# A sequential graph dilation on one core: columns written as turns of the updated rows, and row counts taken from the nearer end

## The chip, the cores and the metric

The kernel runs on one core of one Trainium2 chip. The metric is the time of one execution on the device in microseconds (us); of the kernel before there are three runs. One further execution was recorded by the hardware profiler, and all durations below come from it.

## The reference

Sixteen graphs of 1024 nodes with 128 features pass four graph layers, each followed by a residual add and a layer norm. The change touches only the dilation at the start of the second layer. It walks over the rows of a symmetric 0/1 adjacency and thins each row out; what one row loses, its column loses too, so later rows see what earlier ones did:

```python
def step(carry, n):
    row = jnp.take(carry, n, axis=0)
    nbi = row.astype(jnp.int32)
    num = jnp.sum(nbi)
    sf = jnp.where(num > T_DIL, (num + K_DIL - 1) // K_DIL, 1)   # T_DIL 10, K_DIL 2
    rank = jnp.cumsum(nbi)
    rm = row & (rank % sf == 0)
    valid = (mask_b[n] != 0) & (num > 1)
    rm = jnp.where(valid, rm, False)
    keep = ~rm
    carry = carry.at[n].set(row & keep)
    carry = carry.at[:, n].set(carry[:, n] & keep)
    return (carry, None)
```

A row with more than ten neighbours loses those whose rank is a multiple of half the row's count, rounded up: the middle one, and the last too where the count is even. The thinned adjacency then serves three mean aggregations (SAGE layers); the other three layers use the full one. The mask is all ones in these inputs.

## The kernel before, in words

`fast_kernel` computes the four layers, with tests whose failure sets a flag; a second, general kernel stands behind the flag. In the dilation all sixteen adjacencies lie in SBUF as fp8 (`Y[b]`, 8 row tiles of 128 by 1024 columns, held four matrices to a tile `Yq`). They go in two groups of eight (GB = 8), each prepared in two halves of four (QB = 4). A step is one row tile k of one group g, and there are 16, in the order k, g. A step has three parts:

- `prepare` (from L1033): for each half, VectorE cuts the upper triangle of the diagonal block (`uY`, L1048) and adds up row blocks (`front`, `back`, L1052 to L1058: the sum of three of the first four blocks, or of all four for k of 4 and up, in bf16). TensorE counts into the PSUM tile `s0` (L1066), with the adjacency's column block as the stationary operand and constants (`twos`, `step0`) as the moving one: it gives twice the number of neighbours before a column, and the row's total in column 0. VectorE then makes `sk` (L1069) and small rows: `v1m`, `l1`, `past` (L1070 to L1076).
- `fixed_point` (from L1081): rows of one tile influence each other through the diagonal block. Six evaluations (EVALS = 6) settle how much each row has lost: VectorE marks the hits in `mid` (L1097), TensorE sums them over the rows into `pd` (L1100), VectorE takes the new total `ti` (L1104) and its threshold `thr` (L1092). At the end the diagonal blocks are corrected (L1113) and the per-row numbers `negc` and `wid` made (L1117 to L1130).
- `removal` (from L1132), once for each of the eight members: TensorE counts ranks over the row in two halves of 512 columns, each in its own PSUM bank `s` (L1143). The constant `step`, a triangle of 128 columns followed by 512 twos, is the moving operand; the upper half starts from `front` (and block k where `front` lacks it). ScalarE turns each half into the distance from the middle, `q` (L1145, an absolute value with `negc` as its bias). VectorE compares it with the half width `wid` to get `keep` (L1147) and clears the row by a bitwise and (L1148). Last the column: TensorE copies it in by the identity (L1153) and adds the turned `keep` (L1156), half by half in PSUM `pc`, and ScalarE writes the column back as the positive part of the sum less one (L1157).

The order: `fixed_point` of a step is issued in turns with the `removals` of the step before, an evaluation and then a member, and after four removals half of the `prepare` of the same group's next row tile. The framework's scheduler lays out each engine's queue from this at compile time, and may take ready work of a later part ahead; each engine then runs its queue in order and waits where an operand or a buffer is missing. In the recorded order the rank counts of later members run ahead of the columns of earlier ones. PSUM has eight banks of 512 fp32 columns, all in use here: two for `s0`, one for `pd`, three for `s`, two for `pc`. `q` and `keep` have two buffers, the small rows three. The first four halves are prepared before the loop; the last removals have no evaluation beside them. The stores of matrices 0 to 7 (L1159) close the stage, and the next layer loads them back.

Of the kernel before, what the change touches and what calls it, by code (L numbers as in the profile page):

```python
# [9 lines left out]
F32 = mybir.dt.float32  # L10
F16 = mybir.dt.float16
F32R = mybir.dt.float32r
BF16 = mybir.dt.bfloat16
I32 = mybir.dt.int32
# [625 lines left out]
def fast_kernel(ctx: ExitStack, tc: tile.TileContext, t: dict, out: bass.AP, flag: bass.AP):  # L640
# [221 lines left out]
    step = consts.tile([P, P + 512], BF16, name="step")  # L862
    nc.vector.memset(step, 2.0)
    nc.vector.scalar_tensor_tensor(step[:, :P], upper, 2.0, identb, op0=OP.mult, op1=OP.add)

# [5 lines left out]
    twos = step[:, P:]  # L871
# [3 lines left out]
    off = consts.tile([P, NT, B], F32, name="off")  # L875
    nc.vector.tensor_scalar(off, mok.rearrange("p (b k) -> p k b", k=NT), -1.0, 1.0e5, op0=OP.add, op1=OP.mult)
# [140 lines left out]
    with ExitStack() as ph:  # L1017
        sb = ph.enter_context(tc.tile_pool(name="dl_sb", bufs=2, reuse_waits="tile"))
        small = ph.enter_context(tc.tile_pool(name="dl_small", bufs=3, reuse_waits="tile"))
        ps_b = ph.enter_context(tc.tile_pool(name="dl_pb", bufs=2, space=PSUM, reuse_waits="tile"))  # L1020
        ps_d = ph.enter_context(tc.tile_pool(name="dl_pd", bufs=1, space=PSUM, reuse_waits="tile"))
        ps_s = ph.enter_context(tc.tile_pool(name="dl_ps", bufs=3, space=PSUM, reuse_waits="tile"))
# [8 lines left out]
        def prepare(st, k, g):  # L1031
# [6 lines left out]

            st.front = sb.tile([P, GB, P], BF16, name="front", bufs=3)
            if st.with_last:  # L1040
                st.last = sb.tile([P, GB, P], FP8, name="last")
            for q in range(GB // QB):
# [7 lines left out]
                front = st.front[:, qs, :]  # L1050
                kf = [kb for kb in range(4) if kb != k]
                nc.vector.tensor_tensor(front, Yg[:, :, kf[0], ks], Yg[:, :, kf[1], ks], op=OP.add)  # L1052
                if k < 4:
                    nc.vector.tensor_tensor(front, front, Yg[:, :, kf[2], ks], op=OP.add)
                else:
                    back = sb.tile([P, QB, P], BF16, name="back")
                    nc.vector.tensor_tensor(back, Yg[:, :, kf[2], ks], Yg[:, :, kf[3], ks], op=OP.add)
                    nc.vector.tensor_tensor(front, front, back, op=OP.add)  # L1058
                s0 = ps_b.tile([P, QB, P], F32, name="s0")
                for i in range(QB):  # L1060
                    terms = [(Y[b0 + i][:, kb, ks], P if kb <= k else 1, step0 if kb == k else None)
                             for kb in range(4 if k >= 4 else 0, NT)]
                    if k >= 4:
                        terms.insert(0, (front[:, i, :], P, None))
                    for j, (y, n, m) in enumerate(terms):
                        nc.tensor.matmul(s0[:, i, :n], y, twos[:, :n] if m is None else m,  # L1066
                                         start=(j == 0), stop=(j == len(terms) - 1))
# [686 lines left out]
```

## Time and profile before

| What | us |
|---|---|
| median of three runs (lowest, highest) | 2961.86 (2958.01, 2962.2) |
| the profiled execution's own time | 2964.0 |
| its span, first to last instruction | 2962.2 |
| first evaluation of the dilation starts | 696.2 |
| removals and evaluations together, until the last column is written | about 708 to 1102 |
| end of the evaluations of the first step, of the last | 708.6, 1078.2 |
| busy over the span: TensorE, VectorE, ScalarE | 2725.4, 2196.2, 2024.2 |

The profile's lines are read like this. In a stretch, the busy time of an engine is the time in which at least one of its instructions is in work; a pipelined engine looks busy until the last result is out. A group line names the line of code, engine, operation, output and inputs, shapes and count; behind it stand the summed busy time and the mean of one in ns, and after a second bar the idle time of that engine just before these instructions, with what ended it. A wait is put down to what came last. Consecutive instructions of one engine overlap a little, so an instruction's place in its queue is the distance to the next start and not its duration.

### The profile page before, as it was taken

How to read it: one execution, taken by the hardware profiler on the slowest of the kernel's cores; microseconds unless marked ns; L12 is line 12 of the kernel's file. 1: busy time of each engine (PE TensorE's matmuls, PEld its weight loads, DVE VectorE, ACT ScalarE, POOL GpSimd, SP SyncE). 2: the span in 40 equal slices, each digit the busy share in tenths (PEclk: the TensorE clock that was granted, in tenths of full speed). 3: DMA queues.
4: the chain of work that ended last, by engine and by line, in shares of the span. 5: the costliest groups of instructions: out<-in, count | busy, mean ns of one | idle time of the engine just before them, and what ended most of it. 6: DMA issues, size and time to landing. Idle time of an engine off the chain costs nothing.

```text
span 2962.2 us, 42088 instructions
## 1 busy us (share of the span) xinstructions
PE 2725.4 (92%) x14771; PEld 1695.2 (57%) x14834; DVE 2196.2 (74%) x6087; ACT 2024.2 (68%) x3476; POOL 325.8 (11%) x295
## 2 busy tenths in 40 slices
PE   7999999996999889999899988999999999999996
PEld 3444444443666657877788873555555555555554
DVE  5777777777999976776688785777777777776765
ACT  6788888874788786666555435666666667676753
POOL 0000000030000001111122230001000101000000
PEclk9999999997999999999999997999999999999998
DMA  5444444420000052233467681111111111111000
GB/s 187 135 157 151 163 163 157 151 91 16 2 2 2 2 195 82 100 107 136 162 212 266 228 327 50 47 62 64 61 68 69 60 58 57 57 57 57 22 15 23
DMA packets 124125, 297.91 MB, mean 101 GB/s; under 512 B 12672, under 2 KB 65664, under 8 KB 116736
## 3 DMA queue, kind: packets, MB, share of 16 engines
q1 hardware_dynamic: 103440, 211.65, 21.6%
q0 software_dynamic: 20464, 83.47, 7.1%
q8 instruction: 119, 1.95, 0.3%
q14 instruction: 102, 0.84, 0.1%
HBM read 211.04 MB, written 84.02 MB: 100 GB/s over the span
## 4 chain that ended last, share of the span: by engine, by line
PE 36%; issue 19%; DVE 17%; POOL 4%; ACT 4%; DMA 2%; SPq 0%; POOLq 0%; DVEq 0%; ACTq 0%
PE ph L1550 8%; PE acc L1306 7%; PE ph L766 5%; PE acc L1626 4%; PE ph L1410 3%; PE pmm L724 3%; POOL ln_rstd L745 2%; PE ph L759 2%; DVE ln_st L794 2%; PE ph L1536 2%; DVE em L1612 2%; ACT xn L801 2%; POOL rn L745 1%; DVE A L1679 1%; PE acc L981 1%
## 5 line engine op out<-in xcount | busy, mean ns | idle before, releaser
L724 PE MATMUL pmm<-G,hT 128*128 128x512 f32 x1024 | 512.8, 614 | 10.7 <-DVE mx L1612 6.7
L801 ACT ACTIVATE xn<-xn,ln_nb,ln_rstd 128x128 f32<-128x128 f32 x512 | 207.4, 481 | 112.9 <-DVE ln_nb L799 112.8
L724 PEld LDWEIGHTS pmm<-G,hT 128*128 128x128 f32 x1024 | 175.0, 193 | 166.7 <-issue 118.3
L745 POOL TENSOR_TENSOR ln_rstd<-ln_rstd,mhalf 128x8 f32<-128x8 f32 (+1 forms) x68 | 115.9, 1704 | 1323.9 <-DVE nmx L1614 606.7
L1306 PE MATMUL acc<-a,lo 128*128 128x512 f32 x768 | 243.5, 401 | 15.5 <-DVE lo L1273 15.5
L1626 PE MATMUL acc<-em,hs 128*128 128x512 f32 x512 | 251.8, 611 | 3.5 <-DVE hs L1623 1.9
L981 PE MATMUL acc<-em,hs 128*128 128x512 f32 x512 | 245.7, 601 | 6.5 <-DVE hs L978 5.6
L1306 PE MATMUL acc<-a,hi 128*128 128x512 f32 x768 | 244.1, 402 | 3.7 <-ACT hi L1272 3.5
L1145 ACT ACTIVATE q<-s,negc 128x512 f16<-128x512 f32 x256 | 170.6, 697 | 59.2 <-DVE negc L1124 22.3
L1143 PE MATMUL s<-step,carry 128*128 128x384 bf16 (+3 forms) x1034 | 199.4, 304 | 7.9 <-DVE carry L1113 3.2
L1157 ACT ACTIVATE carry<-pc,negone 128x512 fp8e4<-128x512 f32 x256 | 166.8, 699 | 38.3 <-PE pc L1156 28.9
L972 DVE CUSTOM_DVE_ANT_0 em<-pmm,msk 128x1024 f32<-128x1024 f32 x128 | 155.9, 1218 | 40.6 <-PE acc L981 20.3
L1306 PEld LDWEIGHTS acc<-a,lo 128*128 128x128 f32 x768 | 144.4, 190 | 54.8 <-DVE lo L1273 21.1
L1612 DVE CUSTOM_DVE_ANT_0 em<-pmm,msk 128x1024 f32<-128x1024 f32 x128 | 155.6, 1216 | 25.9 <-PE acc L1626 21.3
L922 ACT ACTIVATE carry<-an 128x1024 fp8e4<-128x1024 f32 x128 | 134.4, 1050 | 50.7 <-DMA an<-in_adj 50.5
L1306 PEld LDWEIGHTS acc<-a,hi 128*128 128x128 f32 x768 | 143.0, 190 | 37.1 <-ACT hi L1272 4.0
L1607 ACT ACTIVATE msk<-A,nbig 128x1024 bf16<-128x1024 fp8e4 x128 | 145.9, 1140 | 26.6 <-DVE mx L1612 23.4
L974 ACT ACTIVATE em<-em,mx 128x1024 f32<-128x1024 f32 x128 | 146.0, 1141 | 25.4 <-DVE mx L972 22.7
L981 PEld LDWEIGHTS acc<-em,hs 128*128 128x128 f32 x512 | 90.9, 189 | 123.9 <-issue 87.2
L1410 PE MATMUL ph<-Wx,hT 128*128 128x128 f32 x768 | 153.4, 282 | 3.0 <-ACT nT L1435 1.4
L1410 PE MATMUL ph<-Wr,ag 128*128 128x128 f32 x768 | 151.1, 279 | 1.4 <-DMA ag<-ag_d 1.2
L1666 ACT CAST A<-A 128x1024 fp32r<-128x1024 fp8e4 x64 | 64.2, 1040 | 124.8 <-PE ph L1550 124.6
(294 smaller groups left out, 6181.9 us busy)
## 6 DMA issues: line engine op xcount, KB each, us to landing
an<-in_adj SPq DMA_DIRECT2D x128, 512.0 KB, 3.5
adj_d<-carry POOLq DMA_DIRECT2D x16, 1024.0 KB, 4.2
A<-dil_d SPq DMA_DIRECT2D x16, 1024.0 KB, 7.1
rdeg<-rdeg_d SPq DMA_DIRECT2D x32, 512.0 KB, 4.2
ag_d<-ag POOLq DMA_DIRECT2D x32, 512.0 KB, 5.3
ag<-ag_d SPq DMA_DIRECT2D x32, 512.0 KB, 6.3
A<-adj_d SPq DMA_DIRECT2D x16, 1024.0 KB, 4.7
xn<-in_x SPq DMA_DIRECT2D x16, 512.0 KB, 4.2
```

The lines of the kernel that those rows point to most:

```text
L724: nc.tensor.matmul(p[:, h * 512:(h + 1) * 512], lhsT, rhs[:, h * 512:(h + 1) * 512], start=True, stop=True)
L745: nc.gpsimd.tensor_tensor(r, r, mhalf[:, :n], op=OP.pow)
L801: nc.scalar.activation(r[:, k.start + i, :], r[:, k.start + i, :], AF.Identity, scale=rstd[:, i:i + 1], bias=nb[:, i:i + 1])
L981: nc.tensor.matmul(s.acc[:, c], hs, em[:, c], start=(jt == 0), stop=(jt == NT - 1))
L1143: nc.tensor.matmul(s[:, lo or 0:], y, twos if lo is None else step[:, :512 - lo], start=(j == 0), stop=(j == len(terms) - 1))
L1145: nc.scalar.activation(q[:, h * 512:(h + 1) * 512], s, AF.Abs, bias=st.negc[:, i:i + 1])
L1157: nc.scalar.activation(Y[b][:, hb, ks], pc, AF.Relu, bias=negone, saturate=False)
L1306: nc.tensor.matmul(acc, part[:, jt, :], pieces[h * NT // 2 + i][:, j, :], start=(jt == 0 and p == 0), stop=(jt == NT - 1 and p == 1))
L1410: nc.tensor.matmul(p[:, i * P:(i + 1) * P], x[:, j * P:(j + 1) * P], W, start=(n == 0), stop=(n == 1))
L1550: nc.tensor.matmul(p, part[:, jt, :], A[:, jt, c], start=(jt == 0 and i == 0), stop=(jt == NT - 1 and i == 1))
L1612: nc.vector.tensor_tensor_reduce(em, e, msk, 1.0, 0.0, op0=OP.add, op1=OP.max, accum_out=mx)
L1626: nc.tensor.matmul(s.acc[:, c], hs, em[:, c], start=(jt == 0), stop=(jt == NT - 1))
```

## The change

- Rank counts of the upper half start at the row's far end: four matmuls of 512, 384, 256 and 128 columns, as in the lower half, with a reversed triangle that is put behind the twos in `step`. ScalarE turns the count around with scale -1 and a second bias, `posc`, which holds `negc` plus twice the row's total `v`. `front` and `back` with all their adds go, and `prepare` counts every block by a matmul of its own.
- A column is made from the updated row: seven matmuls turn the row's other blocks with twice the identity as the moving operand, and only the diagonal block k is still copied in and joined by the turned `keep`. All nine results lie in one `pc` tile of two banks, and one ScalarE instruction of 1024 columns writes the whole column.
- `off`, the term that switches masked rows off (zero here), becomes bf16 and goes into `l1` in one instruction; `v1m` is made from `l1` once for a group, at the start of `fixed_point`; `thr` isn't made anew after the evaluations; `past` is corrected by `off` at the very end.
- PSUM: `s0` has one buffer instead of two, `s` two instead of three, `pc` two of two banks each instead of two of one.

```diff
@@ -859,21 +859,24 @@
     upper8 = consts.tile([P, P], FP8, name="upper8")
     nc.vector.tensor_copy(upper8, upper, saturate=False)
-    step = consts.tile([P, P + 512], BF16, name="step")
+    step = consts.tile([P, P + 512 + P], BF16, name="step")
     nc.vector.memset(step, 2.0)
     nc.vector.scalar_tensor_tensor(step[:, :P], upper, 2.0, identb, op0=OP.mult, op1=OP.add)
+    nc.vector.tensor_scalar(step[:, P + 512:], step[:, :P], -1.0, 2.0, op0=OP.mult, op1=OP.add)
+    identb2 = consts.tile([P, P], BF16, name="identb2")
+    nc.vector.tensor_scalar(identb2, identb, 2.0, None, op0=OP.mult)
     step0 = consts.tile([P, P], BF16, name="step0")
     nc.vector.tensor_copy(step0, step[:, :P])
     nc.vector.memset(step0[:, 0:1], 2.0)
     onec = consts.tile([P, 1], BF16, name="onec")
     nc.vector.memset(onec, 1.0)
-    twos = step[:, P:]
+    twos = step[:, P:P + 512]
     negone = consts.tile([P, 1], F32, name="negone")
     nc.vector.memset(negone, -1.0)
-    off = consts.tile([P, NT, B], F32, name="off")
-    nc.vector.tensor_scalar(off, mok.rearrange("p (b k) -> p k b", k=NT), -1.0, 1.0e5, op0=OP.add, op1=OP.mult)
+    off = consts.tile([P, NT, B], BF16, name="off")
+    nc.vector.tensor_scalar(off, mok.rearrange("p (b k) -> p k b", k=NT), -1.0, 1.0e4, op0=OP.add, op1=OP.mult)
@@ -1017,9 +1020,9 @@
     with ExitStack() as ph:
         sb = ph.enter_context(tc.tile_pool(name="dl_sb", bufs=2, reuse_waits="tile"))
         small = ph.enter_context(tc.tile_pool(name="dl_small", bufs=3, reuse_waits="tile"))
-        ps_b = ph.enter_context(tc.tile_pool(name="dl_pb", bufs=2, space=PSUM, reuse_waits="tile"))
+        ps_b = ph.enter_context(tc.tile_pool(name="dl_pb", bufs=1, space=PSUM, reuse_waits="tile"))
         ps_d = ph.enter_context(tc.tile_pool(name="dl_pd", bufs=1, space=PSUM, reuse_waits="tile"))
-        ps_s = ph.enter_context(tc.tile_pool(name="dl_ps", bufs=3, space=PSUM, reuse_waits="tile"))
+        ps_s = ph.enter_context(tc.tile_pool(name="dl_ps", bufs=2, space=PSUM, reuse_waits="tile"))
         ps_c = ph.enter_context(tc.tile_pool(name="dl_pc", bufs=2, space=PSUM, reuse_waits="tile"))
         def words(v):
@@ -1035,8 +1038,6 @@
             st.sk = sb.tile([P, GB, P], F16, name="sk")
             st.v1m = small.tile([P, GB], F32, name="v1m")
             st.l1 = small.tile([P, GB], F32, name="l1")
-
-            st.front = sb.tile([P, GB, P], BF16, name="front", bufs=3)
             if st.with_last:
                 st.last = sb.tile([P, GB, P], FP8, name="last")
             for q in range(GB // QB):
@@ -1047,33 +1048,17 @@
                 uY = sb.tile([P, QB, P], FP8, name="uY")
                 nc.vector.tensor_tensor(words(uY), words(Yg[:, :, k, ks]),
                                         words(upper8)[:, None, :].to_broadcast([P, QB, P // 4]), op=OP.bitwise_and)
-                front = st.front[:, qs, :]
-                kf = [kb for kb in range(4) if kb != k]
-                nc.vector.tensor_tensor(front, Yg[:, :, kf[0], ks], Yg[:, :, kf[1], ks], op=OP.add)
-                if k < 4:
-                    nc.vector.tensor_tensor(front, front, Yg[:, :, kf[2], ks], op=OP.add)
-                else:
-                    back = sb.tile([P, QB, P], BF16, name="back")
-                    nc.vector.tensor_tensor(back, Yg[:, :, kf[2], ks], Yg[:, :, kf[3], ks], op=OP.add)
-                    nc.vector.tensor_tensor(front, front, back, op=OP.add)
                 s0 = ps_b.tile([P, QB, P], F32, name="s0")
                 for i in range(QB):
-                    terms = [(Y[b0 + i][:, kb, ks], P if kb <= k else 1, step0 if kb == k else None)
-                             for kb in range(4 if k >= 4 else 0, NT)]
-                    if k >= 4:
-                        terms.insert(0, (front[:, i, :], P, None))
-                    for j, (y, n, m) in enumerate(terms):
-                        nc.tensor.matmul(s0[:, i, :n], y, twos[:, :n] if m is None else m,
-                                         start=(j == 0), stop=(j == len(terms) - 1))
+                    for kb in range(NT):
+                        m = step0 if kb == k else twos[:, :P if kb < k else 1]
+                        nc.tensor.matmul(s0[:, i, :m.shape[1]], Y[b0 + i][:, kb, ks], m, start=(kb == 0), stop=(kb == NT - 1))
                 l1 = st.l1[:, qs]
                 nc.vector.tensor_tensor(st.sk[:, qs, :], s0, uY, op=OP.mult)
-                nc.vector.tensor_scalar(st.v1m[:, qs], s0[:, :, 0], 0.5, -1.0, op0=OP.mult, op1=OP.add)
-                nc.vector.tensor_scalar(l1, s0[:, :, 0], -1.0, None, op0=OP.add)
+                nc.vector.scalar_tensor_tensor(l1, s0[:, :, 0], -1.0, off[:, k, gs], op0=OP.add, op1=OP.add)
                 if not st.with_last:
                     nc.vector.tensor_tensor(past[:, k, gs], l1, s0[:, :, P - 1], op=OP.subtract)
-                nc.vector.tensor_add(st.v1m[:, qs], st.v1m[:, qs], off[:, k, gs])
-                nc.vector.tensor_add(l1, l1, off[:, k, gs])
                 if st.with_last:
                     nc.vector.tensor_tensor(st.last[:, qs, :], st.sk[:, qs, :], per_member(l1), op=OP.is_equal, saturate=False)
                 yield
@@ -1085,6 +1070,7 @@
             st.negc = negc = small.tile([P, GB], F32, name="negc")
             st.wid = wid = small.tile([P, GB], F32, name="wid")
             v1m, l1 = st.v1m, st.l1
+            nc.vector.tensor_scalar(v1m, l1, 0.5, -0.5, op0=OP.mult, op1=OP.add)
             ti = small.tile([P, GB], I32, name="ti")
             nc.vector.tensor_copy(ti, v1m)
             for e in range(EVALS):
@@ -1115,13 +1101,13 @@
             v = small.tile([P, GB], F32, name="v")
             nc.vector.tensor_sub(v, l1, ti)
-            thr = small.tile([P, GB], I32, name="thr")
-            nc.vector.tensor_scalar(thr, ti, 1, None, op0=OP.bitwise_or)
             hw = small.tile([P, GB], F32, name="hw")
-            nc.vector.tensor_tensor(hw, thr, ti, op=OP.is_equal)
+            nc.vector.tensor_tensor(hw, thr, prev, op=OP.is_equal)
             nc.vector.tensor_sub(negc, hw, v)
             nc.vector.scalar_tensor_tensor(hw, v, 0.5, hw, op0=OP.mult, op1=OP.mult)
             nc.vector.tensor_sub(negc, negc, hw)
+            st.posc = posc = small.tile([P, GB], F32, name="posc")
+            nc.vector.scalar_tensor_tensor(posc, v, 2.0, negc, op0=OP.mult, op1=OP.add)
             en = small.tile([P, GB], F32, name="en")
             mk = mok[:, g * GB * NT + k:(g + 1) * GB * NT:NT]
             nc.vector.scalar_tensor_tensor(en, v, 10.5, mk, op0=OP.is_gt, op1=OP.mult)
@@ -1136,25 +1122,25 @@
             q = sb.tile([P, N], F16, name="q")
             for h in range(H2):
                 s = ps_s.tile([P, 512], F32, name="s")
-                terms = [(Y[b][:, kb, ks], max((kb - 4 * h) * P, 0)) for kb in range(4 * h, 4 * h + 4)]
-                if h:
-                    terms = [(st.front[:, i, :], None)] + [(Y[b][:, k, ks], None)] * (k < 4) + terms
-                for j, (y, lo) in enumerate(terms):
-                    nc.tensor.matmul(s[:, lo or 0:], y, twos if lo is None else step[:, :512 - lo],
-                                     start=(j == 0), stop=(j == len(terms) - 1))
-                nc.scalar.activation(q[:, h * 512:(h + 1) * 512], s, AF.Abs, bias=st.negc[:, i:i + 1])
+                for j in range(4):
+                    y, w = Y[b][:, 4 * h + (3 - j if h else j), ks], 512 - j * P
+                    if h:
+                        nc.tensor.matmul(s[:, :w], y, step[:, step.shape[1] - w:], start=(j == 0), stop=(j == 3))
+                    else:
+                        nc.tensor.matmul(s[:, j * P:], y, step[:, :w], start=(j == 0), stop=(j == 3))
+                nc.scalar.activation(q[:, h * 512:(h + 1) * 512], s, AF.Abs, scale=-1.0 if h else 1.0,
+                                     bias=(st.posc if h else st.negc)[:, i:i + 1])
             keep = sb.tile([P, N], FP8, name="keep")
             nc.vector.tensor_scalar(keep, q, st.wid[:, i:i + 1], None, op0=OP.not_equal, saturate=False)
             nc.vector.tensor_tensor(words(Y[b][:, k, :]), words(Y[b][:, k, :]), words(keep), op=OP.bitwise_and)
-            for h in range(H2):
-                hb = slice(4 * h, 4 * h + 4)
-                pc = ps_c.tile([P, 4, P], F32, name="pc")
-                nc.tensor.matmul(pc, identb, Y[b][:, hb, ks], start=True, stop=False)
-                for j in range(4):
-                    c = (4 * h + j) * P
-                    nc.tensor.matmul(pc[:, j, :], keep[:, c:c + P], identb, start=False, stop=(j == 3))
-                nc.scalar.activation(Y[b][:, hb, ks], pc, AF.Relu, bias=negone, saturate=False)
+            pc = ps_c.tile([P, NT, P], F32, name="pc")
+            nc.tensor.matmul(pc[:, k, :], identb, Y[b][:, k, ks], start=True, stop=False)
+            nc.tensor.matmul(pc[:, k, :], keep[:, ks], identb, start=False, stop=True)
+            for j in range(NT):
+                if j != k:
+                    nc.tensor.matmul(pc[:, j, :], Y[b][:, k, j * P:(j + 1) * P], identb2, start=True, stop=True)
+            nc.scalar.activation(Y[b][:, :, ks], pc, AF.Relu, bias=negone, saturate=False)
             if k == NT - 1 and b < B // 2:
                 nc.gpsimd.dma_start(dil8_d[b], Y[b].bitcast(F32))
@@ -1710,6 +1696,7 @@
         nc.vector.tensor_tensor(mok, mok, mf, op=OP.not_equal)
         nc.vector.tensor_scalar(zeros, zeros, 0.5, None, op0=OP.is_lt)
+        nc.vector.tensor_sub(past, past, off[:, :NT - 2, :])
         nc.vector.tensor_scalar(past, past, 0.5, None, op0=OP.is_lt)
         nc.vector.tensor_scalar(nodeg, nodeg, 0.5, None, op0=OP.is_lt)
         bms = sb.tile([P, 7], F32, name="bms")
```

## The prediction

> **What bounds the kernel now.** I read the summary page first, then the busy time by stretch, since the change touches one stage of about 394 us (708 to 1102 us) in a span of 2962.2. Columns: length, busy time and instruction count of each engine, granted TensorE clock, DMA share, GB/s.
>
> ```profile
> core 0: us, PE busy (x) PEld busy (x) DVE busy (x) ACT busy (x) POOL busy (x), PEclk, DMA share, GB/s
> 708.00:800.00 92.00, 88.05 (x986) 57.43 (x1004) 84.59 (x245) 72.01 (x116) 0.00 (x0) 0.98 0.01 2
> 800.00:1000.00 200.00, 190.61 (x2105) 124.52 (x2134) 194.69 (x569) 163.62 (x267) 0.00 (x0) 1.00 0.01 2
> 708.00:1102.00 394.00, 369.23 (x4081) 242.51 (x4147) 365.94 (x1054) 315.32 (x514) 4.30 (x8) 0.98 0.09 33
> ```
>
> VectorE is at 97% from 800 to 1000 and 93% over the stage; TensorE looks as busy, but its busy time includes the latency of every burst. So VectorE is the first limit, TensorE close behind, ScalarE at 80% third. Next the groups of instructions inside 708 to 1101 (busy sum and mean duration before the bar's second half, idle before them after it):
>
> ```profile
> L1145 ACT ACTIVATE q<-s,negc 128x512 f16<-128x512 f32 x256 | 170.6, 697 | 59.2 <-DVE negc L1124 22.3 <-PE s L1143 17.2 <-DVE ti L1104 12.8
> L1157 ACT ACTIVATE carry<-pc,negone 128x512 fp8e4<-128x512 f32 x254 | 165.4, 698 | 38.3 <-PE pc L1156 28.9 <-DVE front L1052 3.7 <-DVE ti L1104 2.7
> L1097 DVE TENSOR_TENSOR mid<-sk,thr 128x1024 fp8e4<-128x1024 f16 x90 | 109.7, 1219 | 0.7
> L1156 PE MATMUL pc<-identb,keep 128*128 128x128 bf16 x1020 | 99.1, 220 | 0.5 <-DVE keep L1147 0.4
> L1153 PE MATMUL pc<-carry,identb 128*128 128x512 fp8e4 x256 | 97.2, 380 | 7.2 <-DVE carry L1148 4.2 <-ACT carry L1157 0.9
> ...
> L1147 DVE TENSOR_SCALAR keep<-q,wid 128x1024 fp8e4<-128x1024 f16 x128 | 95.6, 747 | 15.3 <-ACT q L1145 14.9
> ...
> L1052 DVE TENSOR_TENSOR front<-carry 128x512 bf16<-128x512 fp8e4 x28 | 19.1, 684 | 0.1
> ...
> L1057 DVE TENSOR_TENSOR back<-carry 128x512 bf16<-128x512 fp8e4 x16 | 10.9, 681 | 0.0
> ...
> L1058 DVE TENSOR_TENSOR front<-front,back 128x512 bf16<-128x512 bf16 x16 | 6.7, 417 | 0.0
> ```
>
> Nothing waits in front of the front adds: they run back to back in a full queue. The waits of VectorE from 708 to 1081 are short (total us, times, longest):
>
> ```profile
> DVE keep L1147 <- ACT q L1145: 6.2, 9, 2.6
> DVE ti L1104 <- PE pd L1100: 3.9, 7, 1.4
> ```
>
> Last, one evaluation of the fixed point where nothing runs beside it (start, us, engine):
>
> ```profile
> 698.31 1.22 DVE L1097 TENSOR_TENSOR mid<-sk,thr 128x1024 fp8e4<-128x1024 f16 x1
> ...
> 700.41 1.22 DVE L1097 TENSOR_TENSOR mid<-sk,thr 128x1024 fp8e4<-128x1024 f16 x1
> ```
>
> From one mid to the next pass 2.1 us, so an evaluation is a chain of that length, six of them 12.6.
>
> **What the skill says.** (1) The Trainium skill, "TensorE: Matmul & The Clock Gate", section "Wait — 56ns, not 53.3ns?": warm back-to-back matmuls start N/2.4 GHz + 2.5 ns apart, never under about 25 ns. The trace agrees: four 128-column turns take 0.38 us against 0.22 for one, 54 ns apart. (2) "ScalarE: Activation LUTs", "What ACT_TABLE_LOAD costs": about 280 ns + 0.833 ns an element with a bias pointer, neighbours overlapping by 93 ns. 512 columns give 706 by it, 698 here; 1024 give 1133, and rows of that size with a bias take 1140 here. (3) "VectorE: DVE Perf Modes", "Side-by-side": a two-source op runs one element a cycle, two only if all are 16-bit. It fits: 682 ns for the fp8 adds, 417 for the bf16 one. (4) "PSUM — Partial Sum Buffer", "The four PSUM rules": a matmul output fills at most one bank of eight. All eight are taken before (2+1+3+2) and after (1+1+2+4).
>
> **The change part by part.** A step is one row tile k of one group of 8 matrices; 16 steps, first evaluations' ends 708.6 and 1078.2 apart over 15 of them: 24.64 us each, 3.08 a member.
>
> VectorE. An op's queue cost is its spacing to the next, not its duration: the 0.68 us adds stand 0.60 apart, the bf16 one 0.34, tiny ones about 0.09. Front adds removed within 708 to 1101: 28 of L1052, 12 of L1054 (same shape, k below 4), 16 of L1057 at 0.60, 16 of L1058 at 0.34: 16.8 + 7.2 + 9.6 + 5.4 = 39.0 us. Tiny ops: three fewer in each of 28 half-group prepares, 28 x 3 x 0.09 = 7.6. Added per step: v1m and posc, less one thr: 16 x 0.08 = 1.3. Net -45.3, so 365.9 becomes 320.6. Nothing covers this work now; it is on the limiting queue.
>
> TensorE. By columns, a member's removal has 5632 for k below 4 (1280, then 1280 + 1024, then 2 x (512 + 512)), 5120 otherwise; after, 2 x 1280 + 9 x 128 = 3712. Saved: 64 x 1920 + 64 x 1408 = 213,000 columns, 89 us at 2.4 GHz; instructions fall from 20 or 19 to 17. Prepare grows for k of 4 and up from 5 matmuls to 8: 3 x 64 x 0.056 = 11 us. Net about -78, from 347 (columns, plus 25 to 27 ns for each one-column matmul) to 269.
>
> ScalarE. Scale -1 and posc cost what negc did: an immediate and one pointer. Two 512-wide turns (spacing 0.58 where dense) become one of 1024: about 1.14 less 0.11 overlap, 1.03 against 1.16. Saved 0.13, bounds 0.08 to 0.20, times 128: 17 us. 315 becomes 298.
>
> New waits. All nine turns now follow the row's and (L1148, 0.42), where with k of 4 and up the first half waited only for keep; behind those turns in TensorE's queue stand the next counts and the evaluation's pd. An idle of 4.2 us hangs on that now. The ScalarE turn starts only after all nine, 0.50 us. The s bank falls from three to two: exactly one member ahead. s0 falls to one: within the stage its two uses lie four removals apart, so I cost it 0; if that cover goes, it is 0.7 + 0.6 us (sk and the counts) per half-step, 28 x 1.3 = 36. In the prologue (685.8 to 695.6) three trips of TensorE (1.31) and VectorE (about 1.1) take nearly the time that eight adds did: gain 1, bounds -2 to 6.
>
> The sum. A second limit lies close. Over two steps runs a loop: the fixed point's tail to negc (801.8 to 805.3, 3.5), eight removals at ScalarE's 2 x 0.58 + 1.03 = 2.2 each, 3 us for the last one to come through, 2.5 for prepare, then six evaluations, 12.6 alone and some 15 among other work: 39 to 42, or 19.6 to 20.8 a step. VectorE's own work is 320.6/16 = 20.0. Two limits at 20 to 21 don't mesh fully; I take 21.8 a step, between 20.7 (VectorE at 97%, as from 800 to 1000) and 22.6. 15 x (24.64 - 21.8) = 42.6. The drain of the last eight removals follows ScalarE: 8 x 0.13 = 1. With the prologue's 1: -44 or so. Later layers are untouched and start that much sooner: their first loads wait for this stage's stores. The profiled execution took 2964.0 (span 2962.2 and 1.8 around it), so 2920; the median shown is 2961.86, 2 lower, so **2918**.
>
> **The rivals.**
> - Look-ahead lost in part. With two s banks TensorE's in-order queue stands before ScalarE's abs; today only 2.0 us of such wait lie inside the steps. At 0.2 us a member it costs 128 x 0.2 = 26 and leaves 18: 2944. For it: two of three buffered pools shrink. Against: two banks still hold a whole member.
> - TensorE was the real limit, and its 78 us free everything: VectorE at 97% throughout gives 320.6/0.97 = 330, 64 less: 2898. For it: VectorE idles 7.4 of 92 us up to 800, where TensorE has most to do. Against: the loop above.
> - Slower, by lock-step: if the order puts a member's turns ahead of the next one's counts, a member costs its whole chain: counts 0.69, abs 0.70 + 0.58, keep 0.75, and 0.42, turns 0.66, together 3.8, against 3.08 now and 2.73 forecast. It decides from (3.08 - 2.73)/(3.8 - 2.73) = one member in three. At one in two the mean is 3.27: 128 x 0.19 = +24, 2986. Against: counts of later members run before the turns in the present order.
> - Nothing gained: the next layer's first loads (DMA share 0.81 from 1081 to 1102) set the hand-over, not this stage. Against: they read what this stage stores. 2962. Should the new counts not equal the old, the flag would start the second kernel; but the other end's count is twice the total less the old one, and posc is negc plus twice the total, so q is the same.
>
> **How the numbers follow.** Forecast, 30 to 56 us gained: 0.58, own range 2906 to 2932. Look-ahead lost in part, 6 to 30 gained: 0.20. More than 56 gained: 0.07. Nothing: 0.04. Slower: 0.11. Faster by over 0.2% (6 us, about what this kernel's measurement tells from no change): 0.58 + 0.20 + 0.07 = 0.85; same 0.04, slower 0.11. The range leaves out the slower and equal cases and some of the ends: 2902 to 2948.
>
> **What would show it.** Right: no front adds; a step near 22 us; VectorE busy some 320 us in the stage; TensorE's busy time down by far more than the stage; one 1024-wide turn near 1.1 us per member. Wrong: many waits of TensorE's s on ScalarE's q, or of pc on VectorE's and, above 15 us; an s0 wait inside the steps; the stage shorter but the next layer's start not moved.

## The result and the profile after

The changed kernel takes 2906.61 us (median of four runs, 2905.4 to 2911.05) against 2959.94 us before (the three runs named above and one more); the ratio is 0.9822 with a 95% interval of 0.9806 to 0.9839. That is some 53 us or 1.8% faster. The prediction was 2918, with 2902 to 2948 as its range.

Where the time went is found by cutting the span at three events that both kernels have: the end of the first step's evaluations, that of the last step's, and the first matmul of the next layer.

| us in the profiled execution | before | after | difference |
|---|---|---|---|
| end of the first evaluations | 708.6 | 699.6 | -9.0 |
| 15 steps, from there to the end of the last evaluations | 369.6 (24.64 each) | 328.1 (21.87 each) | -41.5 |
| last removals, to the next layer's first matmul | 23.2 | 20.9 | -2.3 |
| all that follows | 1860.8 | 1860.7 | -0.1 |
| span | 2962.2 | 2909.3 | -52.9 |

Nothing is given back later. The busy time by stretch of the changed kernel, with stretches of the same length as those shown before, or the whole stage (length, then busy time and instruction count of TensorE, its weight loads, VectorE, ScalarE and GpSimd):

```profile
699.00:791.00 92.00, 82.36 (x1063) 58.41 (x1065) 86.84 (x253) 77.69 (x104) 0.00 (x0) 0.96 0.01 2
791.00:991.00 200.00, 178.18 (x2376) 130.63 (x2374) 190.09 (x540) 166.12 (x219) 0.00 (x0) 0.99 0.01 2
699.00:1048.00 349.00, 304.92 (x3981) 221.30 (x3985) 323.35 (x910) 290.39 (x384) 4.30 (x8) 0.98 0.09 36
```

VectorE's busy time in the stage falls from 365.9 to 323.4 us, and its share in the middle 200 us is 95%, against 97% before. TensorE, which was level with VectorE, is now well below it. The groups of instructions of the changed kernel from 699 to 1048 us (busy sum, mean in ns, idle before):

```profile
L1143 ACT ACTIVATE carry<-pc,negone 128x1024 fp8e4<-128x1024 f32 x127 | 139.5, 1113 | 22.2 <-PE pc L1142 18.1 <-DVE keep L1134 3.6
L1083 DVE TENSOR_TENSOR mid<-sk,thr 128x1024 fp8e4<-128x1024 f16 x90 | 109.8, 1221 | 0.7
L1134 DVE TENSOR_SCALAR keep<-q,wid 128x1024 fp8e4<-128x1024 f16 x128 | 95.7, 749 | 9.0 <-ACT q L1131 8.7 <-PE pc L1139 0.2
L1131 ACT ACTIVATE q<-s,posc 128x512 f16<-128x512 f32 x128 | 88.2, 689 | 5.8 <-PE s L1128 5.0 <-DVE hw L1115 0.3
L1131 ACT ACTIVATE q<-s,negc 128x512 f16<-128x512 f32 x128 | 88.2, 689 | 37.3 <-PE s L1128 12.6 <-PE pc L1142 10.9 <-PE s L1130 4.0
```

The instructions that stayed cost what they did (`mid` 1221 ns against 1219, `keep` 749 against 747), the reversed counts with their scale of -1 cost ScalarE the same 689 ns as the forward ones, and the column is one write of 1113 ns. No front adds are left. The longest waits of TensorE in its queue, from 699 to 1027 us:

```profile
PE pd L1086 <- DVE mid L1083: 10.3, 18, 1.7
PE s L1130 <- ACT q L1131: 10.1, 21, 1.4
PE s L1128 <- ACT q L1131: 8.3, 17, 0.9
PE s L1128 <- DVE carry L1099: 2.9, 3, 1.6
PE pc L1138 <- DVE carry L1135: 1.2, 3, 0.5
```

TensorE now waits 18.4 us for a free `s` bank (the two lines with ScalarE's `q`), where it waited 2.0 inside the steps before. The wait of the turns for the row's bitwise and, which the change widened, is 1.2 us. VectorE's own waits in the same stretch:

```profile
DVE sk L1057 <- PE s L1055: 4.9, 12, 1.0
DVE ti L1090 <- PE pd L1088: 3.4, 10, 0.9
DVE ti L1090 <- PE pd L1086: 2.8, 13, 0.4
DVE keep L1134 <- ACT q L1131: 1.0, 3, 0.5
```

`keep` waits less for ScalarE than before (1.0 us against 6.2), and `sk` more for the single bank of `s0` (4.9 against 2.3). None of them is long: VectorE is busy for 311.0 of the 328.1 us of the fifteen steps, or 94.8%.

### The profile page after: what moved, and what is told of

Read it like the earlier page. It is cut to its first block, busy times and chain, and to the rows that moved or that the text cites. A ratio compares the mean times of both kernels' runs of the same rounds, so it can differ in the third digit from the quotient of the medians.

```text
span 2909.3 us, 41637 instructions
## 1 busy us (share of the span) xinstructions
PE 2661.7 (91%) x14703; PEld 1675.0 (58%) x14706; DVE 2150.2 (74%) x5930; ACT 2000.8 (69%) x3348; POOL 325.0 (11%) x295
## 4 chain that ended last, share of the span: by engine, by line
PE 39%; DVE 22%; issue 8%; ACT 6%; POOL 5%; DMA 2%; POOLq 0%; DVEq 0%; ACTq 0%; SPq 0%
PE ph L1536 8%; PE acc L1292 6%; PE ph L766 5%; PE acc L1612 4%; PE pmm L724 3%; POOL ln_rstd L745 3%; PE ph L1396 2%; DVE ln_st L794 2%; PE ph L759 2%; PE ph L1522 2%; DVE em L1598 2%; ACT xn L801 2%; POOL rn L745 1%; PE acc L984 1%; PE s L1130 1%
## 5 line engine op out<-in xcount | busy, mean ns | idle before, releaser
L975 DVE CUSTOM_DVE_ANT_0 em<-pmm,msk 128x1024 f32<-128x1024 f32 x128 | 156.0, 1219 | 40.8 <-PE acc L984 19.9
L1593 ACT ACTIVATE msk<-A,nbig 128x1024 bf16<-128x1024 fp8e4 x128 | 145.8, 1140 | 26.5 <-DVE mx L1598 23.3
L1143 ACT ACTIVATE carry<-pc,negone 128x1024 fp8e4<-128x1024 f32 x128 | 140.6, 1113 | 22.2 <-PE pc L1142 18.1
L1602 ACT ACTIVATE em<-em,nmx 128x1024 f32<-128x1024 f32 x128 | 145.6, 1138 | 0.0
L972 ACT ACTIVATE msk<-carry,l0nbig 128x1024 bf16<-128x1024 fp8e4 x128 | 145.0, 1138 | 0.0
```

Of the source, the lines that this page charges most:

```text
L975: nc.vector.tensor_tensor_reduce(em, e, msk, 1.0, 3.0e38, op0=OP.add, op1=OP.min, accum_out=mn)
L1593: nc.scalar.activation(msk, s.A8[:, jt, :], AF.Identity, scale=BIG, bias=nbig, accum_out=zs)
```

## The experiments

Four theories were to be told apart. V, the forecast's: VectorE's queue sets the step. P: TensorE's columns set it. A loop over two steps sets it. And the look-ahead that the PSUM banks allow sets it. The prologue's 9 us were a question of their own. In the table a ratio is to the kernel before, timed together with it; the step and the end of the first evaluations are from the one profiled execution of each.

Two things limit what the small differences say. The framework lays the queues out anew for every kernel. Read from the traces, TensorE's order of work in `room`, `late_bias` and `later_bias` equals that of the changed kernel in 9 to 13 of the fifteen steps (a few matmul records are missing from traces), and in every other kernel of the table in none. So those three add only what they name; in the others a difference is that of the edit together with the order it brought. And a step comes from one execution, which can lie several us off the median of its kernel: the changed kernel's was the slowest of its four (2911.05), that of `later_bias` the fastest of its four (2931.6), and that of `columns_alone` the fastest of twenty (2952.57).

| kernel | median us | ratio, 95% interval | first evaluations end | step |
|---|---|---|---|---|
| before | 2959.9 to 2962.5 | 1 | 708.6 | 24.64 |
| changed | 2906.6 | 0.9822 (0.9806, 0.9839) | 699.6 | 21.87 |
| counts_alone | 2913.5 | 0.9836 (0.9818, 0.9855) | 695.2 | 22.24 |
| columns_alone | 2959.3 | 0.9988 (0.9979, 0.9996) | 708.1 | 24.13 |
| vector_back | 2947.6 | 0.9953 (0.9937, 0.9970) | 710.6 | 23.77 |
| tensor_back | 2929.0 | 0.9879 (0.9861, 0.9896) | 702.9 | 22.96 |
| room | 2916.7 | 0.9850 (0.9833, 0.9868) | 705.0 | 22.08 |
| two_writes | 2916.1 | 0.9844 (0.9825, 0.9862) | 698.4 | 22.23 |
| old_banks | 2907.6 | 0.9816 (0.9799, 0.9834) | 696.1 | 21.65 |
| late_bias | 2919.8 | 0.9853 (0.9835, 0.9871) | 698.9 | 22.26 |
| later_bias | 2936.6 | 0.9918 (0.9903, 0.9933) | 700.7 | 22.95 |
| four_s | 2910.3 | 0.9828 (0.9814, 0.9841) | 698.6 | 21.72 |
| three_pc | 2909.2 | 0.9825 (0.9807, 0.9843) | 698.2 | 21.71 |
| one_pc | 2899.3 | 0.9787 (0.9772, 0.9801) | 697.3 | 21.16 |

### Each half of the change alone

The new counts with the columns as before and the old banks (against the changed kernel, lines on the banks left out):

```diff
-            pc = ps_c.tile([P, NT, P], F32, name="pc")
...
+            for h in range(H2):
+                hb = slice(4 * h, 4 * h + 4)
+                pc = ps_c.tile([P, 4, P], F32, name="pc")
+                nc.tensor.matmul(pc, identb, Y[b][:, hb, ks], start=True, stop=False)
...
```

> The new counts without the new columns: columns half by half from the keep, as before, and the banks of before (two s0, three s, two one-bank pc). VectorE sets the step (theory V, the forecast's): its work falls as in the changed kernel, so the step stays near 22 us (changed kernel 21.87) and the time within 8 us of the changed kernel, 2904 to 2915. TensorE sets the step (theory P): only some 30 of its 78 us are saved, the step is about 23.6 and the time about 2932. The prologue is early in both, since front and back need no room.

The new columns with the counts as before, and the changed kernel's banks (against the kernel before, lines on the banks left out):

```diff
+    identb2 = consts.tile([P, P], BF16, name="identb2")
+    nc.vector.tensor_scalar(identb2, identb, 2.0, None, op0=OP.mult)
-            for h in range(H2):
-                hb = slice(4 * h, 4 * h + 4)
...
+            pc = ps_c.tile([P, NT, P], F32, name="pc")
...
```

> The new columns without the new counts: front and back stay, with the changed kernel's banks (one s0, two s, two two-bank pc). V: VectorE's queue is what it was, the step stays at 24 us or more (before 24.64), the time is 2946 to 2962. P: TensorE saves 48 of 78 us, the step is near 23.0 and the time about 2935. In both the prologue stays late, since front and back keep their room.

The counts alone bring the step to 22.24 us, 2.40 of the 2.77 us that the whole change saves per step; the columns alone save 0.51 in the profiled execution. By the medians they save less: 0.0012 of 2962.5, some 3.6 us for the whole kernel (1.2 to 6.2), which is 0.2 us a step. Both kernels lie where V had them and not where P did. But neither halves the matter cleanly. The counts relieve TensorE too (348.1 to 319.2 us of busy time in the steps), and the columns alone pay with an `s` bank for what they save, so 0.2 to 0.5 us is what is left after that price. Columns alone take 48 us of columns off TensorE and a write per member off ScalarE, and the profile of its steps (708.1 to 1070.1) shows why that buys little:

```profile
708.10:1070.10 362.00, 309.50 (x3773) 217.60 (x3828) 348.60 (x1014) 275.04 (x358) 3.25 (x6) 0.98 0.05 17
```

TensorE has fallen from 348.1 to 309.5 us in these fifteen steps, VectorE has hardly moved (351.1 to 348.6), and it now fills 96% of the time.

### The work put back, engine by engine

The 80 adds computed again, with nobody to use the sums:

```diff
+            st.front = sb.tile([P, GB, P], BF16, name="front", bufs=3)
...
+                front = st.front[:, qs, :]
+                kf = [kb for kb in range(4) if kb != k]
+                nc.vector.tensor_tensor(front, Yg[:, :, kf[0], ks], Yg[:, :, kf[1], ks], op=OP.add)
...
+                    nc.vector.tensor_tensor(front, front, back, op=OP.add)
```

> The changed kernel with the 80 front and back adds computed again, their sums used by nothing. V: the 39 us of adds come back in full, step 24.0 to 24.6, and with the late prologue the time is 2944 to 2958. P: the steps stay within 0.5 us of 21.87 and only the prologue's 9 us come back, 2914 to 2922.

And 896 columns per member put back on TensorE, which the turns then overwrite:

```diff
             pc = ps_c.tile([P, NT, P], F32, name="pc")
+            nc.tensor.matmul(pc[:, 0:4, :], identb, Y[b][:, 0:4, ks], start=True, stop=True)
+            nc.tensor.matmul(pc[:, 4:7, :], identb, Y[b][:, 4:7, ks], start=True, stop=True)
```

> The changed kernel with 896 extra columns per member on TensorE (two matmuls into pc that the turns overwrite), as many as the new columns save: 128 x 0.378 = 48 us more of TensorE, about 317 in all, just under VectorE's 320. V: 0 to 10 us longer, 2906 to 2917. P: 48/78 of the steps' 41.5 us come back, +25, about 2932.

The steps of the two (710.6 to 1067.1 of the first, 702.9 to 1047.3 of the second):

```profile
710.60:1067.10 356.50, 294.73 (x3841) 215.83 (x3841) 343.03 (x946) 273.77 (x359) 3.77 (x7) 0.96 0.05 18
```

```profile
702.90:1047.30 344.40, 324.72 (x4058) 233.04 (x4072) 312.72 (x873) 276.62 (x358) 3.24 (x6) 0.99 0.04 16
```

The adds raise VectorE's busy time in the steps by 32 us (343.0 against 311.0) and the fifteen steps by 28.4. This kernel also has the room of `front` and `back` again, and the next section has a step of 22.08 with that room alone; against it the adds cost 15 x (23.77 - 22.08) = 25 us, so most of it shows. The step is a little under the 24.0 to 24.6 that V gave, the time where V had it. TensorE's extra raises its busy time by 35 us and the steps by 16.3, with VectorE's unchanged. The whole time rises by 0.0057 of 2961 us, 17 us, between the 0 to 10 of V and the 25 of P. So V alone is not the whole truth: with TensorE at 94% and VectorE at 91% of the steps, both engines are felt: 16.3 / 35 is 0.46 us of step for each us put on TensorE, 25 / 32 is 0.8 for VectorE. The extra matmuls stand right in front of the turns, so they lengthen a member's own chain as well as the queue; the two were not told apart. What the change saves in the steps is then VectorE's adds in the main (25 of 41.5 us when they are put back), and TensorE's relief, the single write and the lost banks share the rest.

### The prologue

Nothing in the change was meant to move the start of the stage, and yet the first evaluations end 9 us earlier. The room that `front` and `back` took in SBUF, set aside again:

```diff
+        front_room = sb.tile([P, GB, P], BF16, name="front", bufs=3)
+        back_room = sb.tile([P, QB, P], BF16, name="back")
```

> The changed kernel with the SBUF room of front and back set aside in the stage's pool and nothing else: no instruction more. In the changed kernel the first prepares start inside the last layer's attention (uY at 645.6 against 685.8 us) and the first evaluations end at 699.6 against 708.6. If the freed room lets them start early, they end 7 to 10 us later here, the step stays at 21.9 and the time is 2913 to 2917. If the removed adds themselves made the prologue shorter, nothing changes: within 2 us of 2906.6.

VectorE around the first `uY` (the upper triangle, the stage's first instruction) before the change, after it, and with the room set aside:

```profile
685.75 0.17 DVE L799 SCALAR_TENSOR_TENSOR ln_nb<-ln_mv,ln_rstd 128x8 f32<-128x8 f32 x1 [1.85 <-POOL ln_rstd L745]
685.83 0.28 DVE L1048 TENSOR_TENSOR uY<-carry,upper 128x128 int32<-128x128 int32 x1
```

```profile
645.57 0.27 DVE L1049 TENSOR_TENSOR uY<-carry,upper 128x128 int32<-128x128 int32 x1
645.75 0.28 DVE L981 TENSOR_SCALAR hs<-hn,rs 128x128 f32<-128x128 f32 x1
```

```profile
687.03 0.17 DVE L799 SCALAR_TENSOR_TENSOR ln_nb<-ln_mv,ln_rstd 128x8 f32<-128x8 f32 x1 [1.85 <-POOL ln_rstd L745]
687.12 0.49 DVE L1052 TENSOR_TENSOR uY<-carry,upper 128x128 int32<-128x128 int32 x2
```

With the room taken, not one instruction added, the stage's first instruction stands behind the last norm of the layer before again, as it did before the change; without it, it stands in the middle of the last attention, 40 us earlier. The first evaluations end at 705.0, so 5.4 of the 9.0 us come from the room. The other 3.6 are more than they look, since the last norm itself is 1.3 us later with the room set aside (687.0 against 685.75). From that norm to the end of the first evaluations it takes 22.9 us before, 22.7 in vector_back, which has both adds and room, and 18.0 with the room alone: the adds' going, with the single `s0` bank, is worth 4.9 us. One reason is in the trace: before, the first `mid` (the hits of the first evaluation) stood behind the preparation of all four halves and started at 696.2; with the room alone it starts at 692.1, ahead of the `sk` of the third half (693.2). The time rises by 0.0028 of 2960, 8 us, of which the rest is in the steps: 22.08 against 21.87 with the same instructions. That two executions of the same work, with nothing but the room between them, differ by 0.2 us a step is worth knowing for the small differences below.

### Banks and writes

Columns in two halves written by two ScalarE instructions, from the same banks:

```diff
-            nc.scalar.activation(Y[b][:, :, ks], pc, AF.Relu, bias=negone, saturate=False)
+            for h in range(H2):
+                hb = slice(4 * h, 4 * h + 4)
...
+                nc.scalar.activation(Y[b][:, hb, ks], pc[:, hb, :], AF.Relu, bias=negone, saturate=False)
```

> The changed kernel with the column written by two ScalarE instructions of 512 columns, half by half, from the same two-bank pc: ScalarE gets 128 x 0.15 = 19 us more, 309. V: the step rises by at most 0.3 us, the time by 0 to 5, 2906 to 2912. If the loop over two steps (tail, eight removals at ScalarE's pace, prepare, evaluations) sets the step, 8 x 0.15 / 2 = 0.6 us a step come on top, +9, about 2916.

The same, with `pc` of one bank for each half, and the freed banks back at `s` (three) and `s0` (two):

```diff
-        ps_b = ph.enter_context(tc.tile_pool(name="dl_pb", bufs=1, space=PSUM, reuse_waits="tile"))
+        ps_b = ph.enter_context(tc.tile_pool(name="dl_pb", bufs=2, space=PSUM, reuse_waits="tile"))
-        ps_s = ph.enter_context(tc.tile_pool(name="dl_ps", bufs=2, space=PSUM, reuse_waits="tile"))
+        ps_s = ph.enter_context(tc.tile_pool(name="dl_ps", bufs=3, space=PSUM, reuse_waits="tile"))
...
+                pc = ps_c.tile([P, 4, P], F32, name="pc")
```

> As the kernel with two writes, but pc has one bank per half and the freed banks go back: s has three, s0 two. If look-ahead was lost with the third s bank, it is faster than the kernel with two writes by 5 us or more. If VectorE alone sets the step, the two are within 4 us of each other.

The second write costs 0.36 us a step, between the 0.3 of V and the 0.6 of the loop, and the other banks give back 0.58; 8.5 us in all lie between the two kernels (2916.1 and 2907.6). Which bank does it is open. TensorE's waits from 700 to 1027 us for `s` and for `pc`, with two writes and with the old banks:

```profile
PE s L1130 <- ACT q L1131: 13.5, 30, 1.0
...
PE pc L1145 <- ACT carry L1146: 3.6, 11, 0.7
PE s L1128 <- ACT q L1131: 3.1, 10, 0.6
PE pc L1141 <- ACT carry L1146: 2.8, 7, 0.5
```

```profile
PE s L1128 <- ACT q L1131: 16.3, 29, 1.4
...
PE s L1130 <- ACT q L1131: 2.8, 6, 0.6
```

With the third bank TensorE waits no less for `s` (19.1 us against 16.6); what shrinks is the wait for `pc`, from 6.4 to 0.5 us, and `pc` is here released half by half. So this pair doesn't show that the third `s` bank was worth 0.58. Two more kernels ask which bank counts, and a third tries to have both the single write and the banks.

Banks 1, 4, 2 for `s0`, `s`, `pc`, two writes:

> Columns in two halves, banks one s0, four s, two one-bank pc (the kernel with the old banks has 2, 3, 2). If look-ahead of the rank counts is what the third s bank gave, a fourth gives 0 to 0.3 us a step more against 21.65, and the prologue loses the 3.5 us of the second s0: 2903 to 2911.

Banks 1, 3, 3, two writes:

> Columns in two halves, banks one s0, three s, three one-bank pc. If the turns wait for a free pc bank, the step falls below the 21.65 us of the kernel with the old banks; if the s banks are what counts, it equals it, and with the prologue of one s0 the time is 2908 to 2913.

One write from a single two-bank `pc`, banks 1, 4, 2:

```diff
-        ps_s = ph.enter_context(tc.tile_pool(name="dl_ps", bufs=2, space=PSUM, reuse_waits="tile"))
-        ps_c = ph.enter_context(tc.tile_pool(name="dl_pc", bufs=2, space=PSUM, reuse_waits="tile"))
+        ps_s = ph.enter_context(tc.tile_pool(name="dl_ps", bufs=4, space=PSUM, reuse_waits="tile"))
+        ps_c = ph.enter_context(tc.tile_pool(name="dl_pc", bufs=1, space=PSUM, reuse_waits="tile"))
```

> One ScalarE write of 1024 columns per member as in the changed kernel, but a single two-bank pc, with one s0 and four s. If look-ahead of the rank counts limits the changed kernel more than the second pc, the step falls to 21.3 to 21.7 us, 2896 to 2905, faster than both. If the turns of a member wait for the write of the one before (1.1 us), the step rises by 0.3 us or more, 2911 or above.

With two writes, a fourth `s` bank or a third `pc` bank adds nothing to what the old banks give (21.72 and 21.71 against 21.65); all three have a `pc` of one bank and at least three `s`. With one write, four `s` banks and a single `pc`, the step falls to 21.16 and the kernel takes 2899.3 us, ratio 0.9787 (0.9772 to 0.9801), the fastest of all and clear of the changed kernel's interval. The steps of this kernel, and TensorE's waits in them (to 1014 us):

```profile
697.30:1014.70 317.40, 285.01 (x3849) 212.32 (x3848) 306.23 (x876) 267.40 (x359) 3.53 (x7) 0.96 0.05 18
```

```profile
PE s L1130 <- ACT q L1131: 7.3, 11, 1.2
PE pc L1138 <- ACT carry L1143: 4.4, 9, 1.5
...
PE s L1128 <- ACT q L1131: 1.5, 3, 0.6
```

The wait for a free `s` bank falls from 18.4 to 8.8 us and that for the single `pc` costs 4.4. VectorE fills 96.5% of the steps, against 94.8% in the changed kernel. The code differs from the changed kernel in these two buffer numbers alone, so sharing the banks the other way is worth 0.71 us a step; how much of that is the two buffers themselves and how much the new order of the queues was not tried.

### The loop

`negc` and `posc` copied by GpSimd before ScalarE uses them, once, and then five times in a row:

```diff
+            for name in ("negc", "posc"):
+                for c in range(5):
+                    late = small.tile([P, GB], F32, name=f"late{c}{name}")
+                    nc.gpsimd.tensor_copy(late, getattr(st, name))
+                    setattr(st, name, late)
```

> The changed kernel with negc and posc copied by GpSimd before ScalarE uses them: two small instructions, some 1 to 2 us of delay in each fixed point's tail, no work on a busy engine. If the loop over two steps sets the step, half of the delay comes on every step: 15 x 0.5 to 1.0 = 7 to 15 us longer. If VectorE's queue sets it (V), 0 to 3 us.

> As the kernel with one GpSimd copy, but five copies in a row for negc and five for posc: no work on the three busy engines, and a delay of some 1.5 us for negc and 2.7 us for posc in each fixed point's tail. If the loop over two steps sets the step, half of it shows on every step: 0.75 to 1.35 us, 11 to 20 us in all. If VectorE's queue sets it, the removals only start later and the step stays within 0.3 us of 21.87, 0 to 4 us in all.

One copy raises the step by 0.39 us, which is little more than what room alone did. Five copies say more. GpSimd's timeline in one step, the first and last copy of `negc` and the last of `posc`, and ScalarE's start after `negc`:

```profile
876.46 0.19 POOL L1114 COPY late0negc<-negc 128x8 f32<-128x8 f32 x1 [19.68 <-DVE negc L1108]
...
877.47 0.19 POOL L1114 COPY late4negc<-late3negc 128x8 f32<-128x8 f32 x1
...
878.09 0.23 POOL L1114 COPY late4posc<-late3posc 128x8 f32<-128x8 f32 x1
```

```profile
877.69 0.69 ACT L1136 ACTIVATE q<-s,late4negc 128x512 f16<-128x512 f32 x1 [0.60 <-POOL late4negc L1114]
```

The copies stand 0.25 us apart, so `negc` is late by about 1.25 us in this step; `posc`, whose copies run between those of `negc`, is ready at 876.7 and its last copy ends at 878.3, 1.6 later. In some steps a copy takes longer, and over the fifteen the mean delay is 1.5 us for `negc` and 2.0 for `posc`. The step rises by 1.07 us with no more work on any of the three engines, and VectorE's share falls to 90.5% (311.3 of 344.2 us). So a chain through the fixed point's tail does bind, and V, which allowed 0.3, is not the whole truth here either. The rise is 0.7 of the delay of `negc` and 0.5 of that of `posc`, and it lies within the 0.75 to 1.35 us expected of the loop: half of a delay on every step is not contradicted, and the runs don't say by which of the two numbers to count. The whole time rises by more than the 11 to 20 us expected, by 0.0096 of 2961, 28 us. In the profile 16.1 us of it are in the steps, 1.1 before them and 5.8 behind, where the copies of the last step came 4 us late.

## Why the prediction was right

The forecast was 44 us of gain and the measured 53; the way was right and the size within a fifth. The steps account for 41.5 of the 42.6 us they were to give. That is better than the working deserves: 21.8 was taken between 20.7 and 22.6 and not derived, and the parts behind it missed in both directions.

- **VectorE.** Forecast 365.9 to 320.6 us; measured 323.4. The adds were sized rightly: counting of each instruction only the time after the one before it has ended, the 72 adds in the steps hold 39.9 us of VectorE before, against 39.0 forecast. The Trainium skill, "Vector Engine (DVE) Microarchitecture Reference", section 5.2, gives 1.0417 ns a column and some 75 ns an instruction after overlap; the estimate from it is 608 ns for an add of 512 columns, and in the trace they stand 600 ns apart. What was mis-sized are the small instructions (4 or 8 columns), forecast at -7.6 and +1.3: counted the same way, the 515 of the steps hold 45.9 us before and the 445 that are left hold 45.3. Put back, the adds hold 39.3 us but raise the busy time by 32 only, mostly since the small ones hold 40.9 in vector_back: next to large instructions they take less time of their own.
- **TensorE.** Forecast -78 us of columns; its busy time fell by 64 (369.2 to 304.9), which includes latencies. That this relief is worth less than VectorE's, the forecast's reading, holds, but it is not nothing: 35 us put back cost 16.3 (tensor_back).
- **ScalarE.** Forecast -17, bounds 10 to 26; measured 315.3 to 290.4, -25. One write took 1113 ns and not 1140, and an absolute value 689 and not 697. The single write by itself is worth 0.36 us a step (two_writes).
- **The step.** Forecast 21.8, measured 21.87; 41.5 of 42.6 us. The two limits that were to lie close do: putting work back on VectorE or TensorE, or delay in the tail, lengthens the step. A delay in the tail shows by half to 0.7 on every step, near the half that a loop over two steps gives.
- **The prologue: the step that failed.** "Three trips of TensorE (1.31) and VectorE (about 1.1) take nearly the time that eight adds did: gain 1, bounds -2 to 6." It gained 9.0. Two parts of it were wrong. Without the adds the first evaluation no longer stands behind all four halves, and the prologue is 4.9 us shorter where it starts late (room). And the sum followed the instructions and missed the memory: `front` and `back` took 8 KB per partition, and without them the first instruction runs 40 us earlier. That the stage's tiles then lie where the layer before has already finished is our reading; the addresses were not looked at. The single `s0` bank does cost some time there: the two early kernels with two such banks end their first evaluations at 695.2 and 696.1, the eight early ones with one at 697.3 to 702.9.
- **The drain.** Forecast 1, measured 2.3. Prologue and drain are 9.3 us more gain than the forecast had; the steps take 1.1 back.
- **Waits.** The row's and before the turns: 1.2 us, far under the 15 that were named as a sign of being wrong. The other wait named there, of `s` on ScalarE's `q`, is 18.4 us and over it: that sign came, though the number held. It was costed at 0 with two banks, and the same kernel with four `s` and one `pc` has a step 0.7 us shorter. `s0` with one bank was costed at 0 inside the steps; VectorE waits 4.9 us for it in all, so nearly so.
- **The rivals.** Look-ahead lost in part was put at 0.2 us a member, 26 us in all. The wait it speaks of did grow from 2.0 to 18.4 us, and one_pc bounds its price by some 0.09 us a member (0.71 / 8), if all of that is the banks: it happened, smaller, beside the forecast. Lock-step did not: counts run ahead of the turns, and a member takes 21.87 / 8 = 2.73 us, the value forecast. TensorE as the only limit is spoken against by both halves: columns_alone takes 39 us of its busy time away for 0.2 to 0.5 us a step, and counts_alone reaches 22.24 us with TensorE busy for 96% of the steps (319.2 of 333.6 us). That the hand-over to the next layer gives nothing back is shown by the 1860.7 us behind it.

## What to carry to other kernels

When several engines are near their limit, put the removed work back on one engine at a time: here VectorE's relief, the smaller one, was the larger part of the gain. Ask first whether the experiment kept the order of the queues; where the framework lays them out anew, a small difference has two causes. Sum the memory that an edit frees as well as its instructions, since a stage may then start earlier: 8 KB per partition moved the first instruction here by 40 us. And when two instructions become one that needs more PSUM banks, try more than one way to share them out: one `pc` and four `s` beat two and two by 0.7 us a step.

## What the runs showed of the hardware

A GpSimd copy of 128 x 8 takes 0.19 us in most cases and dependent ones start 0.25 us apart, which makes them a cheap delay to test a chain with; but some of the 160 copies took up to 1.2 us, so the delay has to be read from the trace and not from the count. A ScalarE write of 1024 columns that spans two PSUM banks costs 1113 ns with a bias, 0.8 of two writes of 512 (2 x 698), and a scale of -1 costs nothing (689 ns both ways). Small VectorE instructions (4 or 8 columns) hold 0.09 to 0.10 us of its time each, and taking 70 of them out of 515 freed 0.6 us in all.
